# Two-layer image kernel: groups of 20, 7, 3 and 2 images instead of 21, 8 and 3, the last group's spectra kept on chip, and statistics sums started two rounds ahead

## The chip, the cores and the metric

The kernel runs on one core of a Trainium2 chip. The core has a matrix engine (TensorE, PE in the profile; PEld is its weight load), a vector engine (DVE), a scalar engine (ACT), GpSimd (POOL) and a queue engine for transfers (SyncE, SP).[...] The metric is the device time of one execution in microseconds (us); lower is better. The profile is one execution taken by the hardware profiler.

## The reference, cut to what matters

Two layers, each of the form x + f(normalised x), on 32 images of 32 channels of 128x128 numbers in float32.

```python
# layer 0: _gn normalises over groups of 2 channels; then, for each 128x128 matrix A,
Y = A / normA;  Z = I
for _ in range(5):
    T = 0.5 * (3.0 * I - Z @ Y);  Y = Y @ T;  Z = T @ Z
x = x + Y * sqrt(normA)
# layer 1: _gn again, then
x_dht = fftn(v, axes=(2, 3)).real
top = einsum('bixy,ioxy->boxy', x_dht[:, :, :32, :32], weights1)
bot = einsum('bixy,ioxy->boxy', x_dht[:, :, -32:, :32], weights2)
out_dht = zeros; out_dht[:, :, :32, :32] = top; out_dht[:, :, -32:, :32] = bot
x = x + ifftn(out_dht, axes=(2, 3)).real
```

Layer 0 is a matrix iteration on 1024 matrices. Layer 1 keeps 64x32 frequencies of a transform, mixes the 32 channels with a weight matrix of its own at each frequency (the weights are 8 MB in all), and transforms back.

## The kernel before

**Layer 0.** The unit of work is a set: 4 channels of one image, a tile of 128 partitions x (4 x 128). There are 8 sets to an image, 256 in all. `newton` (L393) is a generator that takes one set through its chain of products; one call of `products` (L297) is 4 matmuls of 128x128x128, recorded as 8 (two records to a float32 matmul). A set has 11 such calls, and `transposed` (L303), 4 transposes on TensorE, one to three times. For the images called far (`is_far`, L309: images 1 to 19) `quartic` (L357) does its transpose on DVE in blocks of 32 and through DRAM (the tile `turn`); for the near ones (0 and 20 to 31) it does it on TensorE. FIRST (L50), which sets the limit, is the first group's size less one.

**Rounds.** The main loop (L876) is written out at build time. In a round it goes once over 9 lanes (LANES); each lane holds a set and takes it on by one `yield`. A new set starts every 3 rounds (far) or 5 (near). The code of the engines' queues comes from the order in which this loop emits, rearranged by a planner except where an instruction is marked `kept`. Side queues of generators are stepped once a round or less: `preps` (statistics of the input for layer 0's normalisation, `prep` L180), `posts` (at lane 3: `settle` L419 stores a finished set to DRAM as `mid`, folds it on POOL and takes its moments; `forward` L436 transforms 8 folded tiles' rows on TensorE), `specs` (at lane 2: `spectrum` L475 does the column transform, the second layer's statistics through `moments` L157 and two matmuls at L509 and L512, and stores the scaled spectrum `spec` to `xs` in DRAM), `prods` (two rounds in three) and `backs` (the third).

**Layer 1's mixing.** Images are mixed in groups, GROUPS (L41), so that a weight that is loaded serves many images. When a group's last spectrum is done, `follow` (L859) queues its mixing on `prods` and its images' `inverse` (L726) on `backs`; a group's inverses begin when `prods` is empty (`finish`). The first group, of 21, is mixed by `wide_products` (L545), 32 steps of 16 matmuls that stream 128 columns. Groups of up to 8 go through `small_products` (L601): 16 steps (one for each kk, with its 512 KB of weights) of 32 matmuls that stream 32 columns, with the spectra read back from `xs` (L622), copies of the PSUM result to `om` (L667) and stores of it to `od` in DRAM (L631). A group smaller than 8 copies and stores `om` in four parts. `inverse` loads `od` (L688) and `mid` (tile `yt`, L703), reorders (L736), multiplies (L748, L770), copies the sine part to `d` (L782), adds on DVE (L787), adds and subtracts on POOL (L723), and stores the image (L711).

**The end.** When no set is left (`tail`), every queue is stepped at every lane, half of L723 goes to DVE, and the sets' tiles are released, so that 14 of the 16 weights can be loaded to tiles of their own by POOL's queue (L886).

**The statistics' waits.** In `moments`, `prep` and `spectrum` a small matmul sums over the partitions what DVE has just made: L167 (`ms`), L206 (`q` of `prep`), L509 (`qr`). Between DVE's instruction and the matmul stands one `yield`, so one round. `forward` has none between POOL's folds and its matmuls (L447) but the one at the end of `settle`.

## Time and profile before

| | |
|---|---|
| median of 3 runs | 3196.84 us (3196.34 to 3201.53) |
| span of the profiled execution | 3205.1 us, 78907 instructions |
| DMA | 637.55 MB, mean 199 GB/s |
| matmuls of the sets, L300 | 8 groups of the page's part 5, 2048 or 4096 records each |
| last L413, the end of layer 0's last set | begins 3081.36 us |
| column transform of images 0, 1, 18, 19, 20, 21 (L484 begins) | 159.6, 259.4, 1714.5, 1789.0, 1871.8, 1983.5 us |
| the same of images 26, 27, 28, 29, 30, 31 | 2555.2, 2669.8, 2777.2, 2895.5, 3004.5, 3088.1 us |
| `wide_products` on TensorE (L581) | 1895.8 to 2048.6 us |
| `small_products` of the group of 8 and of the group of 3 (L652) | 2803.5 to 2877.4 us; 3112.7 to 3149.9 us |
| inverses of the group of 21 begin (L748) | 2058 to 2736 us, one every 34 us |
| inverses of the group of 8 begin | 2888 to 3115 us |
| inverses of the group of 3 begin | 3161.7, 3171.7, 3184.8 us |

The columns of a profile line are read as follows. In the table of stretches: the stretch, its length, busy time and instructions of each engine, the granted TensorE clock as a share of full speed, the share of the DMA engines and the GB/s they moved. In the list of waits: who waited for whom, the us in total, how often, and the longest. In the chain of work that ended last: start, length, what. In the timeline: start, length, engine, line, operation, output and inputs, count, and in brackets the idle time before it with what ended it. Several waits for different engines overlap, and a wait of an engine that is not the bound costs nothing.

### The profile page before, as it was taken

The numbers are of one execution on the slowest core, as the hardware profiler recorded it, in microseconds if no ns is written. First come the engines' busy times: TensorE is split into PE (matmuls) and PEld (weight loads), VectorE is DVE, ScalarE is ACT, GpSimd is POOL, SyncE is SP. The second block draws the span as 40 slices with busy tenths as digits, with TensorE's granted clock in tenths as the row PEclk, the third lists the DMA queues.
The fourth block names the chain that finished last, engine by engine and source line by source line (L and its number), as shares of the span: only waits on it lengthen the run. The fifth ranks groups of instructions, "written<-read, shape, count | busy, mean of one in ns | idle before, by whom it ended". The sixth has DMA issues, their size and how long they took to land.

```text
span 3205.1 us, 78907 instructions
## 1 busy us (share of the span) xinstructions
PE 2973.7 (93%) x29440; PEld 2850.6 (89%) x29440; DVE 2316.5 (72%) x5158; ACT 1701.5 (53%) x4148; POOL 2003.6 (63%) x2314
## 2 busy tenths in 40 slices
PE   6999999999999999999999999999999898999964
PEld 6899989999999999999999998889888888998953
DVE  5777777778778877788777765677776776756645
ACT  3555556565556555656655454455455454536533
POOL 3566666667667766667666443476767666646742
PEclk9999999999999999999999999999999999999975
DMA  3566666666666666666665346766676566476577
GB/s 126 164 204 193 202 187 199 208 202 212 199 200 213 196 201 190 202 201 208 211 198 159 96 148 206 221 219 216 214 232 219 194 231 206 160 224 212 187 264 232
DMA packets 482317, 637.55 MB, mean 199 GB/s; under 512 B 97936, under 2 KB 263056, under 8 KB 481936
## 3 DMA queue, kind: packets, MB, share of 16 engines
q1 hardware_dynamic: 366592, 413.82, 40.6%
q10 hardware_dynamic: 113328, 211.34, 21.2%
q0 software_dynamic: 2016, 7.34, 0.6%
q8 instruction: 235, 3.85, 0.5%
q14 instruction: 146, 1.20, 0.1%
HBM read 398.75 MB, written 233.57 MB: 197 GB/s over the span
## 4 chain that ended last, share of the span: by engine, by line
PE 68%; DVE 12%; DMA 11%; issue 3%; POOL 3%; ACT 2%; SPq 1%; ACTq 0%; DVEq 0%; POOLq 0%
PE ps L300 55%; PE ps L306 6%; DMA xs<-in_xt 4%; DMA w<-turn 2%; DVE turn L366 2%; PE ps L770 2%; PE ps L447 1%; DVE v L275 1%; DVE a_st L195 1%; POOL yt L723 1%; DVE q L275 1%; DMA yt<-mid 1%; PE ps L748 1%; DVE yt L787 1%; PE ps L581 1%
## 5 line engine op out<-in xcount | busy, mean ns | idle before, releaser
L381 POOL TENSOR_TENSOR w<-w,r 128x512 f32<-128x512 f32 x304 | 386.5, 1275 | 352.0 <-DMA w<-turn 300.9
L300 PE MATMUL ps<-w,v 128*128 128x128 f32 x4096 | 556.2, 280 | 8.9 <-POOL w L381 3.6
L334 ACT ACTIVATE b<-b,a_off,a_scr 128x128 f32<-128x128 f32 x1024 | 470.1, 490 | 144.5 <-issue 48.6
L300 PE MATMUL ps<-y,q 128*128 128x128 f32 x4096 | 531.2, 278 | 11.8 <-ACT d L782 9.9
L300 PEld LDWEIGHTS ps<-w,v 128*128 128x128 f32 x4096 | 506.2, 195 | 13.3 <-POOL w L381 5.8
L300 PEld LDWEIGHTS ps<-y,q 128*128 128x128 f32 x4096 | 496.6, 195 | 16.0 <-ACT d L782 10.4
L426 POOL TENSOR_TENSOR fold<-xt 128x256 f32<-128x256 f32 x512 | 363.6, 730 | 217.7 <-DVE xt L413 194.4
L275 DVE SCALAR_TENSOR_TENSOR q<-ps,eye 128x512 f32<-128x512 f32 x512 | 349.2, 682 | 174.4 <-PE ps L300 168.6
L723 POOL TENSOR_TENSOR yt<-yt,d 128x512 f32<-128x512 f32 x238 | 299.9, 1287 | 177.6 <-ACT d L782 132.2
L341 POOL TENSOR_SCALAR x<-xt,a_nm,a_sc 128x128 f32<-128x128 f32 x720 | 315.5, 450 | 20.4 <-DVE a_n L224 20.4
L409 ACT ACTIVATE y<-ps,a_t_s 128x128 f32<-128x128 f32 x1024 | 291.3, 368 | 63.6 <-PE ps L300 63.1
L195 DVE BATCH_NORM_STATS2 a_st<-xs 128x6 f32<-128x128 f32 x1024 | 227.2, 279 | 134.3 <-DMA xs<-in_xt 133.7
L294 POOL TENSOR_TENSOR r<-mb,eye 128x512 f32<-128x512 f32 x104 | 132.5, 1274 | 304.4 <-ACT mb L269 298.9
L300 PE MATMUL ps<-x,b 128*128 128x128 f32 x2048 | 279.4, 280 | 5.7 <-POOL x L341 5.6
L269 ACT ACTIVATE t<-ps 128x512 f32<-128x512 f32 x256 | 152.5, 596 | 247.6 <-PE ps L300 240.6
L366 DVE STREAM_TRANSPOSE turn<-v 128x512 f32<-128x512 f32 x304 | 277.6, 913 | 5.3
L300 PE MATMUL ps<-m,q 128*128 128x128 f32 x2048 | 280.1, 281 | 0.5 <-DVE q L275 0.5
L300 PE MATMUL ps<-m,mb 128*128 128x128 f32 x2048 | 280.2, 281 | 0.1
L300 PE MATMUL ps<-y,t 128*128 128x128 f32 x2048 | 277.4, 279 | 2.7 <-ACT d L782 1.4
L300 PE MATMUL ps<-x,q 128*128 128x128 f32 x2048 | 277.8, 279 | 1.9 <-DVE q L275 1.9
L413 DVE TENSOR_TENSOR xt<-ps,xt 128x512 f32<-128x512 f32 x256 | 175.4, 685 | 143.6 <-PE ps L300 141.0
L300 PE MATMUL ps<-q,t 128*128 128x128 f32 x2048 | 275.6, 278 | 0.0
(124 smaller groups left out, 5827.2 us busy)
## 6 DMA issues: line engine op xcount, KB each, us to landing
turn<-turn SPq DMA_DIRECT2D x304, 256.0 KB
b<-in_x ACTq DMA_DIRECT2D x256, 256.0 KB
xt<-in_xt ACTq DMA_DIRECT2D x256, 256.0 KB
xs<-in_xt ACTq DMA_DIRECT2D x256, 256.0 KB
mid<-xt SPq DMA_DIRECT2D x256, 256.0 KB
yt<-mid SPq DMA_DIRECT2D x128, 512.0 KB
out<-yt SPq DMA_DIRECT2D x109, 512.0 KB
w<-turn SPq DMA_DIRECT2D x152, 256.0 KB
```

Of the source, the lines that this page charges most:

```text
L195: nc.vector.bn_stats(st[:, 4 * i + c, :], tiles[i][:, c, :])
L275: nc.vector.scalar_tensor_tensor(s, ps, f, t, ALU.mult, ALU.add)
L300: nc.tensor.matmul(ps[:, j, :], lhsT[:, j], rhs[:, j], start=True, stop=True)
L306: nc.tensor.transpose(ps[:, j, :], t[:, j, :], ident)
L334: nc.scalar.activation(t, x, AF.Identity, bias=offset[:, c], scale=scale[:, c])
L341: nc.gpsimd.tensor_scalar(m[:, j, :], xt[:, j, :], nm[:, c // 2 : c // 2 + 1], sc[:, c : c + 1], ALU.add, ALU.mult,)
L366: nc.vector.transpose(blocks(t), v.rearrange(form, b=4))
L381: nc.gpsimd.tensor_tensor(w, w, r, ALU.add)
L409: nc.scalar.mul(y[:, j, :], py[:, j, :], sn[:, c : c + 1])
L413: nc.vector.tensor_tensor(xt, products(t, y), xt, ALU.add)
L426: nc.gpsimd.tensor_tensor(f[:, :, 64 * half : 64 * half + 64], xt[:, :, 0:64], xt[:, :, 64:128], op)
L723: engine.tensor_tensor(yh, yh, d, op)
```

## The change

It has four parts.

1. **Groups.** GROUPS becomes (20, 7, 3, 2). The group of 3, mixed after the last set until now, is mixed while sets are still under way, and only two images are left for after. Image 19 becomes near, for FIRST falls from 20 to 19.
2. **The last group.** Its spectra don't go to DRAM. Eight copies, on ACT and DVE by turns, lay each `spec` out in `diags` as a stationary operand that is block-diagonal in l (4 blocks of 32 channels); 32 of its columns are 2 images x 4 values of l x 4 frequencies. `last_products` streams past them the weights of the same four frequencies at once, 4 x 32 columns: 128 matmuls of 128 columns instead of 512 of 32. Of the 4 x 4 pairs of frequencies that this forms, the stores pick the four that match. Its results are copied to `om`, stored in 16 transfers on two queues, and read back by `inverse`, which splits its reordering between ACT and DVE. It also loads the first of the two images' `mid` ahead.
3. **Late weights.** While the last set is under way, 28 half weights of 256 KB are loaded on SP's queue to tiles of the sets as these come free (`weights`, with the round from which each tile may be taken). The release of the sets' tiles and POOL's loads go.
4. **Sums two rounds ahead.** The one `yield` before L167, L206 and L509 becomes two. The second layer's statistics become a generator of their own, `summed`, that is queued right after the last `settle` of an image, ahead of `forward`; `spectrum` takes up its result. `forward` begins with a `yield`.

```diff
-GROUPS = (21, 8, 3)
+GROUPS = (20, 7, 3, 2)
...
         nc.vector.tensor_reduce(ms, f[:, :, :, 1], AX.X, ALU.add)
-        yield
+        yield from pause
         pm = bank()[:, 0, 0:G]
...
+    pause = (None, None)
...
-        yield
+        yield from pause
         pq = bank()[:, 0, 0:C]
...
     def forward(b, q, u):
+        yield
...
+    def summed(b, st):
+        ms, _, d = yield from moments(st, "b")
+        yield
...
+        yield from pause
+        pv = bank()[:, 0, :]
...
+        scales[b] = v, r
+        yield
...
+        v, r = scales.pop(b)
         ps = transposed(z)
...
+        if i == len(xs):
+            for e, t in enumerate(diags):
+                for l4 in range(4):
+                    rows = slice(32 * l4, 32 * l4 + 32)
+                    copy = nc.scalar.copy if l4 % 2 else nc.vector.tensor_copy
+                    copy(
+                        t.rearrange("p (m b l f) -> p m b l f", b=2, l=4, f=4)[rows, :, j, l4, :],
+                        spec[rows, 8 * e : 8 * e + 8].rearrange("p k q (h f) -> p (k q h) f", f=4),
+                    )
+            yield
+            return
...
+        if i == len(GROUPS) - 2:
+            for t in diags:
+                nc.gpsimd.memset(t, 0.0)
+            for kk in range(2):
+                load_weights(kk)
...
+    def last_products(i):
+        for e in range(2):
+            load_input(B - GROUPS[i], e)
+        for kk in range(KK):
+            if kk % 4 == 0:
+                yield
+                om = page(f"om{i}_{kk}").rearrange("p (f s o) -> p s f o", f=4, s=8)
+            if kk % 2 == 0:
+                pm = bank()
+            for h in range(2):
...
+                for q in range(4):
+                    m = 8 * (kk % 8) + 2 * q + h
+                    nc.tensor.matmul(
+                        pm[32 * q : 32 * q + 32, 2 * (kk % 2) + h, :],
+                        diags[kk // 8][:, 32 * m : 32 * m + 32],
+                        wt[:, q, :],
...
+            if kk % 4 == 3:
+                for f in range(4):
+                    queue = nc.scalar if f % 2 else nc.sync
...
+    def weights():
+        kinds = [("b", 2)] * 3 + [("x", 2), ("b", 4), ("x", 4), ("x", 10), ("y", 10), ("y", 10)]
+        kinds += [("m", 11)] * 2 + [("r", 12)] * 4 + [("mb", 15)] * 2 + [("v", 15)] * 2
+        kinds += [("w", 16)] * 2 + [("y", 16), ("m", 16), ("r", 17)] + [("q", 19)] * 3
...
-            if late and turn % 2:
-                y = late[0].tile([P, 8, P], F32, tag="yt_late", name=f"yt{b}_{o}", bufs=8)
+            if len(settled) == B * C // 4 and not folds and turn % 3 == 2:
+                y = sets.tile([P, 8, P], F32, tag="fold", name=f"yt{b}_{o}", bufs=3)
...
+            if where[b][0] == len(GROUPS) - 1:
+                for h, copy in enumerate((nc.scalar.copy, nc.vector.tensor_copy)):
...
+        if g == C // 4 - 1:
+            posts.append(then(summed(b, st)))
         if g % 4 == 3:
             posts.append(forward(b, g // 4, u))
...
-        if tail and not posts and not late:
-            phase.close()
-            late.append(ctx.enter_context(tc.tile_pool(name="late", bufs=1)))
-            for kk in range(2, KK):
-                late_wts.append(late[0].tile([P, 2, 4, 4, C], F32, name=f"wt{kk}_late"))
-                nc.gpsimd.dma_start(out=late_wts[-1], in_=wk[kk])
...
             step(norms)
+            step(loads)
...
+                if not todo:
+                    loads.append(weights())
```

## The prediction

> **What bounds the kernel now.** I read the page's busy shares, then a table of stretches, then TensorE's waits, then the chain of waits after layer 0's last set. The table of stretches first:

> ```profile
> 60.00:1680.00 1620.00, 1565.95 (x13867) 1519.38 (x13867) 1273.12 (x2862) 948.27 (x2343) 1087.37 (x1209) 0.98 0.64 198
> 1680.00:1900.00 220.00, 217.09 (x1990) 210.55 (x1989) 153.61 (x362) 111.36 (x269) 126.43 (x164) 1.00 0.39 119
> 2060.00:2800.00 740.00, 690.99 (x6637) 657.12 (x6635) 538.39 (x1168) 371.11 (x928) 504.96 (x594) 0.97 0.64 211
> 2880.00:3060.00 180.00, 174.12 (x1735) 165.54 (x1737) 115.92 (x212) 106.12 (x240) 121.92 (x140) 1.00 0.63 200
> 3082.00:3113.00 31.00, 7.90 (x88) 5.02 (x84) 10.36 (x25) 4.55 (x11) 12.39 (x19) 0.56 0.92 336
> 3113.00:3154.00 41.00, 21.31 (x1083) 19.12 (x1071) 20.23 (x28) 12.61 (x26) 5.44 (x4) 0.62 0.50 153
> 3154.00:3173.00 19.00, 8.14 (x74) 7.76 (x76) 3.10 (x5) 6.00 (x8) 0.98 (x1) 0.50 0.87 225
> 3173.00:3205.00 32.00, 11.74 (x122) 9.85 (x119) 27.33 (x32) 9.91 (x25) 16.65 (x12) 0.61 0.88 310
> ```

> There are two kernels here. Up to 3082 us PE (first busy figure) is 93 to 99% busy and its weight loads 89 to 96%, no other engine is over 79%: PE is the bound, so each us of PE work added costs about one, and each us of PE standing still that goes is about one gained. After 3082 PE is a quarter to a half busy, at little over half clock: the last 123 us are a chain of waits. What PE waits for between 60 and 3060 us:

> ```profile
> PE ps L206 <- DVE a_qs L201: 34.9, 16, 8.9
> PE ps L509 <- DVE b_qr L504: 14.9, 7, 3.1
> PE ps L447 <- POOL fold L426: 12.9, 7, 4.4
> ...
> PE ps L206 <- DVE b_r_q L150: 7.1, 2, 3.7
> PE ps L206 <- DVE b_inv L521: 5.2, 2, 3.2
> ```

> With two smaller rows (L206 4.4, L167 1.2) the statistics' matmuls and the folds hold PE for 80.6 us, out of some 125 us. The chain after the last set, its longest pieces:

> ```profile
> 3095.96 13.49 DMA xs<-spec
> 3114.96 1.57 SPq L622
> 3119.61 4.36 DMA diag<-xs
> ...
> 3129.39 6.84 DMA od<-om
> 3139.48 4.14 DMA od<-om
> ...
> 3159.80 12.91 DMA yt<-mid
> ```

> The spectra's way through DRAM takes from 3095.96 to the first product at 3112.73 (it shares the DMA engines with POOL's 7.3 MB of weights: 336 GB/s), the products to 3152.7, held by SP's loads and stores, then results and `yt` come back until 3172.7. The three images go at DVE's pace: `yt` L787 and L723 repeat every 11 us (3173.8, 3184.7, 3195.6).

> [...] The trace shows 0.50 to 0.62 in the tail, and the 24 records of L770 take 2.2 us there against 1.2 before. [...] In the trace 32 records of L581 (128 rows by 32, 128 columns) take 1.11 us, where 32 of L300 take 3.6, so three to four at once. [...]the 24 KB stores `od<-om` land in 1.5 us, which I use.

> **The change part by part, layer 0's stretch.**
> *Sums two rounds ahead.* A far round lasts 86 us / 24 = 3.6 us (an image every 86 us, 8 sets of 3 rounds), a near one 110 / 40 = 2.8. The mean wait is 51.6 / 22 = 2.3 us at L206, 2.1 at L509, 1.8 at L447. One round more covers nearly all of them (not the 8.9 us one). Behind the waiting matmul stands all of PE's queue, so the gain is direct, where PE has other work. DVE may still lag: bounds 30 and 80 us, I take 70%, **-56**. The added yield of `forward` hides in the spacing of sets, and `summed` ends about when the spectrum is through; no cost.
> *Image 19 near.* 16 more calls of `transposed`; eight records of L306 stand in the chain with 1.02 us, so 0.5 us a call, 8 us of PE. Against it a far image leaves PE idle 3% of 86 us, and image 20, near and without layer 1 beside it, took 82.8 us where images 1 to 18 took 86.4 each. Bounds 0 and 8, **+5**. DVE and POOL are relieved.
> *The group of 3 mixed earlier.* 16 steps of 64 records at 1.07 us (L652 at full clock): **+17**. Its loads, stores and copies, 16 x 0.58 us ACT and 16 x 0.69 DVE, the four-part copies of the group of 7, and one more pair of memsets (3.6 us POOL) lie on engines 60 to 75% busy: nothing.
> *Two more inverses before the end* (30 instead of 28): 1.09 + 2 x 1.19 us of PE each: **+7**.
> *The drain.* At 3068 to 3075 PE waited for `gt`, which stood on ACT behind L736's 5.7 us wait for `or<-od`. In the new order the group of 3's inverses end earlier: image 29 is 80 rounds before the end, 11 go to its spectrum, 26 to 16 product steps (2803 to 2877 us), 3 x 12 to the inverses. 7 are left. **-3**.
> Sum -30: the last L413 ends at 3052 instead of 3082.1.

> **The tail**, counted from that end (before: 123.0 us).
> *To the spectrum* it took 13.9. The fold no longer stands behind POOL's `yt` (0.9), and the scale is there when `z` is transposed (2.6 between that and L526): 10.4.
> *Lay-out in `diags`:* eight copies of 32x256, four each on ACT and DVE; the nearest row is `d` L782, 128x256, 384 ns: 1.8. At 12.2 (before: first product at 30.6).
> *Products:* 256 records. At 32 in 0.84 us (1.11 less one latency of 0.27) 6.7 us at full clock, 13.5 at half. They are dense[...]: 10. At 22.2. PSUM copies (16 halves, two engines) keep up. The weights, 7.3 MB at 250 to 336 GB/s or 22 to 29 us, are issued from the last set's start, some 40 us before its end: hidden.
> *Store and read back:* copy 0.7, issue 0.6, landing 1.5 to 3[...], 2.2: 25.7. Loads 1.2 to issue and, from 3154.5 to 3159.8, 5.3 with `yt` beside them, without 3: 29.9. L736 takes 1.92 whole, half on each engine 1.1: 31. `yt` of the first image is there.
> *Two images:* L748 2.1, `gt` 1.1, first L770 2.3, then 2 x 11 on DVE, 1 for its part of L736, the last L723 1.9, the last stores 4.6: 35. **66** in all, so **-57**. Bounds 58 and 80.

> Span 3052 + 66 = 3118. The profiled execution is 8.3 us above the median, so **3110 us**.

> **Rivals.** *A: the waits only move.* DVE is 73 to 79% busy[...]; its sums come behind `v`, `turn` and `yt`, and PE freed of one wait may meet another. For it: some twenty other kinds of waits stand in the list. Against: none sums over 12 us, and in 1680 to 1900 us PE is 99% busy. Then the main stretch gains nothing: 3110 + 56 = 3166. *B: work spills into the tail.* If an inverse takes 13 rounds, not 12, or the last half weights (those for `q` come only at round 19 of the last set's 23) land late, the tail keeps 10 to 25 us: about 3128. *C: slower.* `page` has three buffers for `om`, `d` and `or`, and more mixing now goes on beside inverses. In the tail of before ACT stood 5.7 us at `d` for `od<-om`. Were that so at each of the 16 store steps of the groups of 7 and 3, ACT and then PE would lose 91 us, and SP's queue, held by a half weight whose tile is not free, another 10 with the `mid` stores behind it: 3110 + 101 = 3211. Against it: by the cadences (20 inverses of 34 us; spectra 110 us apart) products and inverses overlap only some 30 to 60 us in all.

> **How the numbers follow.** My forecast 0.54, A 0.2, B 0.18, C 0.08. Low end: all waits recovered (-24) and the tail at 58 (-8): 3078. High end: A with a little of B, 3172. Faster by over 0.2% (below 3190): 0.91; within 0.2% 0.02; slower 0.07, from C and its near cases.

> **What would show it.** Right: PE's waits at L206, L509 and L447 sum to under 25 us between 60 us and the last L413; that L413 ends near 3052; no `xs<-spec` in the tail; the first product 12 us after it, the last 22 after; first L748 at 31; two images 11 us apart; end at 66. Wrong: PE as idle in 60 to 3040 us as before under other names (A); L748 of image 29 after the last L413, or products waiting for weights (B); ACT idle before `om` or `d` with a DMA as releaser between 2500 and 3000 us (C). The forecast also falls if TensorE stays at half clock and streams one column tile at a time in the products: 256 records at 0.22 us (twice the 0.11 of an L300 record in a full row) would be 56 us.

## The result and the profile after

The kernel after takes 3104.59 us in the median of 4 runs (3097.7 to 3112.25) against 3196.59 before: a ratio of 0.971 with a 95% interval of 0.9682 to 0.9737. The forecast was 3110 us. Its profiled execution spans 3098.6 us, of before 3205.1, so the trace shows 106 us where the medians show 92: that of before is of an execution some 8 us above the median, that of after of one some 4 us below. Executions of the kernel after lie up to 15 us apart, and differences below are taken from spans that end at a marked instruction.

That mark is the end of layer 0's last set: line L413 before, L420 after. It falls from 3082.1 to 3035.0 us (forecast 3052), and the tail behind it from 123.0 to 63.6 us (forecast 66). The table of stretches of the kernel after (stretch, length, busy us of PE, PEld, DVE, ACT and POOL with counts, granted clock, DMA share, GB/s):

```profile
60.00:1600.00 1540.00, 1519.98 (x13658) 1476.73 (x13657) 1250.88 (x2820) 927.98 (x2291) 1068.95 (x1191) 0.99 0.67 204
1600.00:1770.00 170.00, 166.98 (x1584) 161.18 (x1583) 114.02 (x256) 82.22 (x199) 88.80 (x122) 0.99 0.36 108
1935.00:2600.00 665.00, 634.05 (x6927) 603.02 (x6926) 514.36 (x1083) 343.52 (x856) 468.35 (x547) 0.99 0.71 233
3034.00:3048.40 14.40, 6.44 (x44) 3.87 (x43) 4.99 (x22) 4.27 (x10) 2.78 (x4) 0.63 0.78 290
3048.40:3062.00 13.60, 8.63 (x256) 8.39 (x256) 3.05 (x5) 2.93 (x6) 0.00 (x0) 0.88 0.20 41
3062.00:3070.90 8.90, 2.08 (x16) 1.79 (x16) 1.20 (x2) 2.00 (x2) 0.00 (x0) 0.50 0.81 209
3070.90:3098.60 27.70, 9.68 (x112) 8.25 (x112) 19.80 (x24) 7.14 (x21) 11.75 (x8) 0.56 0.50 199
```

In the far stretch PE is now 98.7% busy (96.7% before), and its granted clock is 0.99 instead of 0.98. In the tail the 41 us of products of before have become 13.6, in which the clock rises to 0.88. TensorE's waits from 60 us to the mark, of the kernel after:

```profile
PE ps L307 <- DVE w L282: 9.8, 7, 2.5
PE ps L307 <- DVE q L282: 7.9, 6, 2.9
PE ps L307 <- ACT d L893: 7.6, 3, 4.3
PE ps L307 <- POOL w L388: 7.5, 6, 3.8
PE ps L859 <- ACT ob L847: 6.4, 2, 4.3
...
PE ps L455 <- POOL fold L433: 1.0, 1, 1.0
...
PE ps L213 <- DVE a_qs L208: 0.8, 1, 0.8
```

The statistics' matmuls (L213 is L206 of before) and the folds (L455, before L447) held PE for 80.6 us and hold it for 2.0. But the whole list has fallen by 42 us only, from 127.7 to 85.3: other waits have grown, chiefly those for the sets' own `w` and `q`. Part of that comes with the new groups, which alone let TensorE stand 10 us longer (e2 below).

Some pieces of the chain of waits of the tail:

```profile
3046.14 1.18 ACT spec L541
...
3048.44 3.44 PE ps L723 x64
...
3060.04 2.16 DMA od<-om
...
3065.02 5.58 DMA yt<-mid
...
3084.49 2.48 DVE yt L898 x4
```

No `xs<-spec` stands in it any more: the first product (L723) begins 2.3 us after L541, which scales the spectrum, the last one is done at 3057.1, the results are back at 3067.3, and DVE works off the two images.

### The profile page after: what moved, and what is told of

Its sections match the earlier page's. It is cut to its first block, busy times and chain, and to the rows that moved or that the text cites. A ratio compares the mean times of both kernels' runs of the same rounds, so it can differ in the third digit from the quotient of the medians.

```text
span 3098.6 us, 79471 instructions
## 1 busy us (share of the span) xinstructions
PE 2948.7 (95%) x29760; PEld 2828.6 (91%) x29760; DVE 2340.0 (76%) x5178; ACT 1704.0 (55%) x4153; POOL 1998.0 (64%) x2312
## 3 DMA queue, kind: packets, MB, share of 16 engines
q14 instruction: 145, 1.19, 0.1%
## 5 line engine op out<-in xcount | busy, mean ns | idle before, releaser
L388 POOL TENSOR_TENSOR w<-w,r 128x512 f32<-128x512 f32 x288 | 366.3, 1276 | 324.3 <-DMA w<-turn 274.8
L827 POOL TENSOR_TENSOR yt<-yt,d 128x512 f32<-128x512 f32 x248 | 311.2, 1282 | 153.7 <-ACT d L893 116.0
L301 POOL TENSOR_TENSOR r<-mb,eye 128x512 f32<-128x512 f32 x112 | 142.7, 1274 | 311.3 <-ACT mb L276 298.8
L348 POOL TENSOR_SCALAR x<-xt,a_nm,a_sc 128x128 f32<-128x128 f32 x736 | 322.7, 451 | 19.5 <-DVE a_n L231 19.5
L373 DVE STREAM_TRANSPOSE turn<-v 128x512 f32<-128x512 f32 x288 | 262.0, 910 | 4.6
L307 PEld LDWEIGHTS ps<-m,q 128*128 128x128 f32 x2048 | 251.6, 193 | 10.7 <-DVE q L282 5.8
```

Source lines behind the costliest of these rows:

```text
L301: nc.gpsimd.tensor_tensor(r, mb, eye, ALU.add)
L307: nc.tensor.matmul(ps[:, j, :], lhsT[:, j], rhs[:, j], start=True, stop=True)
L348: nc.gpsimd.tensor_scalar(m[:, j, :], xt[:, j, :], nm[:, c // 2 : c // 2 + 1], sc[:, c : c + 1], ALU.add, ALU.mult,)
L373: nc.vector.transpose(blocks(t), v.rearrange(form, b=4))
L388: nc.gpsimd.tensor_tensor(w, w, r, ALU.add)
L827: engine.tensor_tensor(yh, yh, d, op)
```

## Experiments

Three quantities are needed for them that no view gives ready made. **Standing** is the length of the stretch from 60 us to the mark less TensorE's busy time. **Clock loss** is what the granted clock below 1 takes in it: over stretches of 5 us, the sum of 5 us x (1 - granted clock). What is left of the stretch is **work**, at full clock. In us:

| kernel | mark | standing | clock loss | work | tail |
|---|---|---|---|---|---|
| before | 3082.1 | 128.5 | 58.4 | 2835 | 123.0 |
| e1: before, two yields at the sums | 3010.1 | 83.3 | 34.0 | 2833 | 129.6 |
| e2: before, new groups | 3115.8 | 138.7 | 47.8 | 2869 | 101.0 |
| e9: before, image 19 near | 3074.2 | 119.8 | 49.5 | 2845 | 129.2 |
| after | 3035.0 | 86.5 | 27.2 | 2861 | 63.6 |
| e5: after again | 3043.5 | 90.5 | 30.7 | 2862 | 63.0 |
| e3: after, one yield at the sums | 3120.3 | 142.7 | 56.4 | 2861 | 62.2 |
| e7: after, no yield in `forward` | 3066.8 | 109.3 | 32.5 | 2865 | 63.4 |
| e12: after, two more rounds | 3023.5 | 80.6 | 18.7 | 2864 | 62.5 |

The work column supports the method: it hardly changes with the yields, and steps by some 30 us with the groups. Standing and clock loss overlap where the clock is low while TensorE stands, by 2 to 8 us in these traces, so work is too low by as much. Each row is one trace. Up to the mark, after, e4, e5, e6, e8, e10 and e11 differ by a few transfers at most, and over these seven the mark lies between 3032.8 and 3047.5 us, standing between 85 and 95 and clock loss between 25 and 34: smaller differences than these show nothing.

### e1 and e3: the sums alone, from both sides

```diff
# e1, in the kernel before, at L165, L204 and L507
-        yield
+        yield from pause        # pause = (None, None)
# e3, in the kernel after
-    pause = (None, None)
+    pause = (None,)
```

e1:

> The kernel before with one edit only: two yields instead of one ahead of L167, L206 and L509 (no other order, no forward yield). Theory (the standing of TensorE at the sums is the main stretch's gain, and comes back nearly whole): waits at L206, L509 and L167 fall from 68 us to under 10, TensorE idle in 60 to 3060 us falls by 35 or more, and its busy time at the same work falls by 10 to 30 us because the granted clock rises from 0.98 to 0.99; the time falls by 45 to 75 us, to 3122 to 3152. Rival (the waits only move, and the gain of layer 0's stretch came from the new groups): idle falls by under 15 us, the time is 3180 to 3195.

e3:

> The kernel after with pause = (None,), so one yield again ahead of the three sums; summed ahead of forward, and forward's yield, stay. Theory: the waits at the sums are back with 50 us or more, the granted clock falls to 0.98, the time rises by 40 to 65 us to 3145 to 3170. Rival (the new groups made the gain): under 15 us, 3105 to 3120.

e1 took 3141.42 us, 0.9811 of before (0.9786 to 0.9836), as the theory had it; e3 3190.75, 0.9974 (0.9959 to 0.9988), 20 us more than the top of its range. Taking the second yield out again gives back 86 us of the change's 92. TensorE's waits in e3:

```profile
PE ps L213 <- DVE a_qs L208: 46.8, 23, 8.2
PE ps L307 <- DVE w L282: 12.9, 7, 4.2
...
PE ps L498 <- DVE b_qr L493: 7.4, 5, 3.0
```

and in e1:

```profile
PE ps L307 <- ACT sw L465: 26.5, 18, 3.8
PE ps L448 <- POOL fold L427: 9.9, 8, 3.3
```

So the yields do what they were meant to. In e1 65 us of waits at the sums go, but the wait for `sw` (in `forward`) grows from 3.5 to 26.5 us, and standing falls by 45: a third of it moves. In e3 56 us of waits at the sums come back and standing rises by 56: in the order of the kernel after nothing moves. The mark falls by 72 us in e1 and rises by 85 in e3 (73 to 88 against the seven marks named above). Clock loss supplies most of the rest: 24 and 29. How a stand costs clock is seen in the kernel before, in TensorE's timeline and in stretches of 5 us (busy, count, granted clock, DMA share, GB/s):

```profile
635.76 0.61 PE L206 MATMUL ps<-a_qs,avg_mean 128*128 128x32 f32 x2 [3.19 <-DVE b_inv L521]
...
639.63 1.91 PE L300 MATMUL ps<-x,b 128*128 128x128 f32 x8
```

```profile
625.00:630.00 5.00, 5.00 (x47) 1.00 0.68 224
630.00:635.00 5.00, 2.57 (x24) 1.00 0.30 83
635.00:640.00 5.00, 4.24 (x20) 0.52 0.38 125
640.00:645.00 5.00, 5.00 (x38) 0.80 0.40 126
```

TensorE stands 3.19 us; its granted clock is then 0.50 for 6.8 us (635.15 to 641.98 us), and eight records of L300 take 1.91 us instead of 1.06. The two pieces below 1 lose 3.4 us of clock, nearly all of it on top of the 3.2 us of standing. Not every stand does this: of the 25 of 2 us or more in the stretch before, 24 were followed by half clock, of the 35 of 0.5 to 2 us only 2; after, 11 of 17 and 2 of 32. Over the whole stretch before, 36 of 604 such 5 us pieces are below 0.9; after, 19 of 595.

### e2: the groups alone

```diff
-GROUPS = (21, 8, 3)
+GROUPS = (20, 7, 3, 2)
```

> The kernel before with one edit only: GROUPS = (20, 7, 3, 2); the last two spectra still go through DRAM and the late weights still come on POOL's queue. Theory (the prediction's +29 us of TensorE work before the end is real): the last L413 ends 20 to 30 us later than 3082; the tail loses one image (11 us) and what spilled into it, and is 95 to 110 us long instead of 123; the time is 3195 to 3210, no gain. Rival (regrouping costs layer 0's stretch nothing, since far image 19 was as dear as a near one): the last L413 ends at 3080 to 3090 and the time is 3170 to 3185.

3223.71 us, 1.007 of before (1.0045 to 1.0096): slower by 0.7%, and by more than expected. The mark is 33.7 us later, work is 34 us more, and the tail, one image shorter, is 101.0 us. The new groups alone lose; they pay only with what the last group's new way takes off the tail, 39 us more (e3's tail of 62.2, with the same groups).

### e9: image 19 near

```diff
-        return 0 < b < FIRST
+        return 0 < b < FIRST - 1
```

> The kernel before with image 19 near (is_far up to FIRST - 1), nothing else. Theory (prediction: 8 us of TensorE work less what the far image stands idle): busy time of TensorE to the last L413 plus 7 to 8 us, that L413 0 to 10 us later, the time 3197 to 3210. Rival (near images beside nothing else are faster than far ones, as image 20's 82.8 us against 86.4 looks): the last L413 3 to 6 us earlier.

3214.88 us, above its range, and 1.003 of before (1.0006 to 1.0055), which is 2 to 18 us more. In the trace work is 10 us more, standing and clock loss together 18 less, so the mark came 8 us earlier, which is within the spread of marks of one kernel, and the tail was 6 longer. But this trace is of one of the three shortest of the twelve executions (3205 us). The work is about as priced (8 us). That a far image stands more is suggested by this one trace, not shown, and what image 19 costs in the end isn't settled.

### e4 and e6: late weights and the way through DRAM

```diff
# e4: in weights(), ahead of the loads; the yield after each load goes
+        while todo or any(lanes):
+            yield
# e6: in spectrum, ahead of the lay-out in diags
+            kept(nc.sync.dma_start(out=there, in_=spec.rearrange(flat)))     # a tile in DRAM
+            spec = sp.tile([P, 4, P], F32, tag="sp", name=f"back{b}", bufs=2)
...
+            kept(nc.sync.dma_start(out=spec.rearrange(flat), in_=there))
```

e4:

> The kernel after with its 28 half weights issued only once the last set has left its lane, all in a row. Theory (in the kernel after they are hidden behind the last set): 7.3 MB at 340 GB/s is 22 us and the last ones are wanted some 20 us after the last L413, so the products wait: they end 5 to 15 us later, 3110 to 3120. Rival (the early loads slow the last sets as much as they save): same as after, 3100 to 3108.

e6, and e5 as its base:

> The kernel after with each of the last two spectra stored to a tile in DRAM and loaded back before it is laid out in diags; all else as it is. Theory (the way through DRAM is worth little once 7 MB of weights no longer stand before it): a store and a load of 256 KB on idle DMA engines are 2 to 3 us each, so the tail grows by 5 to 7 us, where the prediction put the first product 18 us earlier. Rival (the DRAM way itself was the 13 us of before): plus 13 to 18 us.

> The kernel after, unchanged, as the base for the runs beside it. Expected: last L420 at 3030 to 3040 us of its span, a tail of 62 to 66 us, 0.971 of the kernel before.

e5 gave 3103.92 us, 0.9698 (0.9672 to 0.9724). e4 gave 3113.15 us, 0.9719 (0.9688 to 0.975), so the intervals overlap, but the tail of its trace is 80.7 us against 63.6, and TensorE's timeline says where (in brackets the idle time before, and what ended it):

```profile
3064.08 0.43 PE L723 MATMUL ps<-v,diag 128*32 128x128 f32 x8 [2.22 <-DMA v<-in_wk]
...
3072.81 0.66 PE L723 MATMUL ps<-q,diag 128*32 128x128 f32 x8 [1.19 <-DMA q<-in_wk]
```

From 3064 us on the products wait for half weights; they end 35.6 us after the mark instead of 22.1, and the stores follow. So in this trace hiding the weights is worth 17 us of tail, and in that of the kernel after no product waits for them. But the trace is of the slowest of e4's four executions (3121 us; two others took 3107), and by the medians e4 is 9 us longer: 17 is the upper end. e6 gave 3106.79 us, 0.971 (0.9685 to 0.9734): not to be told from e5 by the clock, but the tail is 68.2 us against 63.0, and its chain shows the way through DRAM at its own price:

```profile
3045.90 2.04 DMA there<-spec
3047.99 2.74 DMA back<-there
```

That is 5 us for both ways, where in the kernel before the store `xs<-spec` alone took 13.5 us beside 7.3 MB of weights. Keeping the spectra on chip is a small part of the tail's gain.

### e7: forward's yield

```diff
     def forward(b, q, u):
-        yield
```

> The kernel after without the yield at the start of forward. Theory (TensorE stood 12.9 us at the folds before, and each stand of 2 us also costs clock): waits at L455 (here L454) come back with 8 to 13 us, and the last L420 ends 8 to 18 us later. Rival (summed, now ahead of forward, already takes the place of that yield): no change over 3 us.

3129.31 us, 0.9781 (0.9756 to 0.9807), 25 us more than e5. TensorE's waits:

```profile
PE ps L313 <- ACT sw L471: 14.5, 13, 2.9
PE ps L454 <- POOL fold L433: 13.2, 10, 3.9
PE ps L307 <- ACT d L892: 13.0, 7, 4.3
```

The folds are back with the expected 13 us; `sw` and `d` rise too, so the mark moves by 23 to 32 us, more than expected. The prediction had put this yield at no cost and had counted its gain inside the 80.6 us; taken out alone, it costs 25 of the 95 us. The parts don't add up, for e3 alone costs 86.

### e8, e10 and e11: the last images

```diff
# e8 and e11
-            engine = nc.vector if tail and o % 16 else nc.gpsimd
+            engine = nc.vector if tail and o == 24 else nc.gpsimd
# e10 and e11: out stores on nc.sync; both images' mid loaded at the start of last_products
-            kept((nc.scalar if tail else nc.sync).dma_start(out=out[b, :, o : o + 8, :], in_=y))
+            kept(nc.sync.dma_start(out=out[b, :, o : o + 8, :], in_=y))
```

> The kernel after with one of four L827 pairs on DVE in the tail (o == 24) instead of two. Theory (DVE sets the pace of the last images, 11 us each, 5.0 at L898 and 5.6 at L827): DVE has 7.8 us an image, POOL 8.8, so an image takes 9 us and the tail is 3 to 5 us shorter. Rival (POOL becomes the bound, or the wait for d): no shorter, or longer by up to 3.

> The kernel after with the last images' stores on SP's queue instead of ACT's, and the mid of both last images loaded at the start of last_products. Theory (DVE's 10.6 us an image is the bound of the last 28 us): the L842 copies come 1 to 2 us sooner, for fewer loads stand beside or, and the tail is 1 to 3 us shorter. Rival (ACT's standing before d, 3.5 us twice, behind a store that waits for L827, is the bound): 4 to 7 us shorter.

> The same, and one of four L827 pairs on DVE instead of two (as in e8_unfold_share). Theory (in that run POOL and DVE were paced by d, whose copies stood behind ACT's stores): now POOL 8.8 us an image, the tail is 4 to 7 us shorter than that of after (63 us), the time 3096 to 3101. Rival: POOL's longer list ends later, tail 61 to 64 us.

They gave 3103.08 us (0.9695, 0.9669 to 0.9721), 3110.94 (0.9695, 0.9648 to 0.9743) and 3102.11 (0.9673, 0.9628 to 0.9719), with tails of 64.7, 64.9 and 63.3 us: nothing gained in any, where e8 and e10 were expected to shorten the tail and e11 by 4 to 7 us. In e8 ACT's copies to `d` stood behind its own stores, which waited for POOL:

```profile
ACT d L893 <- POOL yt L827: 5.8, 2, 3.1
```

In e11 that was gone and DVE was through with the two images in 16 us instead of 20, but POOL's twelve operations ended later than DVE, and `or` came 1 us later. The tail's last part is shared so closely by DVE, POOL and ACT that moving one piece didn't shorten it in these three.

### e12: the same remedy at two more places

```diff
         nc.scalar.copy(sw, ps)
-        yield
+        yield from pause
...
                     obs[b].rearrange("p (l t o) -> p o t l", l=4, t=8),
                 )
+                holding.append(b)
+                yield
+                holding.pop()
```

> The kernel after with one round more at two further stands of TensorE: between sw (L472) and its transposes in forward, and between L847's reordering of ob and its matmuls in the inverses of the groups of 7 and 3 (stepped in the next round). Theory (a stand costs its length and nearly half of it again in granted clock, and a round more removes it): the 6 to 15 us of waits at L313 for sw and L859 for ob go, the last L420 ends 8 to 20 us sooner than after's 3035 to 3047, the time is 3085 to 3100. Rival (by now the waits move: other engines' order is what TensorE waits for): these waits go, others come, the time stays within 5 us of 3104; the inverses, a round longer, may spill into the tail.

3091.45 us, 0.9654 of before (0.9628 to 0.968). Its six executions (3079.64 to 3096.84) all lie below the six of e5 (3099.59 to 3108.47), though the two intervals of the ratio touch. The wait for `sw` has left the list, that for `ob` is halved:

```profile
PE ps L862 <- ACT ob L847: 3.2, 2, 2.8
```

Some others are a little higher (`d` 9.5, `w` 11.8), and standing fell by 6 to 10 us. Clock loss fell by 8 to 12: 7 stands of 2 to 3 us are left, of 11 in the kernel after and 10 in e5. Mark, standing and clock loss all lie below the ranges of the seven traces named above. The mark is 11 to 20 us earlier, and the version beats both kernels by the median.

## Why the prediction was right, and where not

Direction and time came as forecast, and so did the tail: -57 was said and -59 measured. For layer 0's stretch -30 was said and -47 measured (-39 in e5). These -47 us are 26 of work more, 42 of standing less and 31 of clock loss less; the forecast had +29 for the groups, -59 for standing and nothing for the clock. That the time came within 6 us is partly luck: the forecast took the profiled execution to be 8.3 us above the median, and that of after lies 4 below, so that by spans it was 19 us off (3118 against 3098.6).

1. **Sums two rounds ahead, -56.** This is the term that was mis-sized. The mechanism is shown by e1 and e3: -72 and 85 us. "One round more covers nearly all of them" held: 80.6 us of waits became 2.0. "So the gain is direct, where PE has other work" was too small a sum. Standing itself moved by 45 us in e1, where a third of it came back at `sw` (rival A, in part), and by the forecast 56 in e3. But the stands had cost clock as well, 24 to 31 us in all, which the prediction left out: it had reckoned with half clock in the tail only, while the trace of before already showed a granted clock of 0.98 in the stretch. It had also put `forward`'s yield at no cost and no gain of its own, and without it 25 us are lost (e7).
2. **Image 19, the group of 3 and two more inverses, +29.** Work rose from 2833 to 2835 us to 2861 to 2865, by 26 to 32: as summed. e2 puts it at 34. Image 19's share was priced about right as work (10 us for 8); its net cost isn't settled.
3. **The drain, -3**, can't be told apart. The last inverse before the tail begins at 3012.8 us (L859), 22 us before the mark, and POOL's last L827 ends 0.5 us after it, so next to nothing spilled (rival B didn't happen).
4. **To the spectrum, 10.4.** It took 12.6. "The scale is there when `z` is transposed" was right, but the statistics' matmuls stand ahead of the column transform (L523 begins 7.3 us after the mark, 6.0 before): L498 waits 1.5 us for `b_qr`, and the transform stands behind it on PE.
5. **Products, from 12.2 to 22.2.** They ran from 13.5 to 22.1. The first 64 records took 3.44 us at a mean granted clock of 0.56, the other 192 some 5.2 at 1.00. That the clock would rise within the products was an estimate of mine: 10 us, between 6.7 at full clock and 13.5 at half. The weights were hidden: no product waited for one.
6. **Store and read back, to 31.** The results were reordered at 33.4: ACT's two stores of each four, 0.6 and 0.85 us to issue, stand between its copies.
7. **Two images, 35.** 30.3 from L859 on: DVE took 10.6 and 9.3 us for them. The reading that the way through DRAM had cost 18 us was too large as a cause: by itself it costs 5 (e6). That the rest was the weights beside it is argued, not shown, for no run of the kernel after has both. The sum of the step didn't change by that.
8. **Rival C**, ACT held by transfers of `om`, didn't come: from 2500 to 3000 us ACT waited 19.8 us for `or`, and under 2 for each other transfer.

What was not tried by itself: the new place of `summed` ahead of `forward`, the dense products without SP's loads and stores, and the first image's `mid` loaded ahead. If the parts add, the last two are the 15 us of the tail that one image less (22, e2), the weights (17, e4's trace) and the spectra (5) leave, or 23 with the 9 us of e4's medians.

## What to carry to other kernels

Where TensorE is the bound, list what it stands for by name, and give a matmul that needs another engine's small result one more slot of distance in the order of emission; a regrouping that shortens the tail can cost more in front than it saves, so price both sides at full clock. Count standing at about one and a half times its length (e1: 45 us of standing and 24 of clock), but as a mean: in the kernel before 24 of the 25 stands of 2 us or more were followed by half clock, of the 35 of 0.5 to 2 us only 2. After such a repair look at the list again: part of the standing may have moved (a third in e1), and the same remedy worked once more at two other places (e12).

## What the runs showed of the hardware that I had not expected

In the kernel before a stand of TensorE of 3.19 us in a stretch that is otherwise fully busy was followed by half clock (granted clock 0.52 and 0.80 in two pieces of 5 us), and so were 24 of the 25 stands of 2 us or more. The prediction had reckoned with half clock in the tail only. Over layer 0's stretch the clock loss was 58 us of the kernel before and 19 us of e12; of the 58, some 6 us fall in time in which TensorE stands.

| busy in the step | steps | the next one at half clock |
|---|---|---|
| under 40% | 25 | 25 |
| 40 to 50% | 16 | 10 |
| 50 to 65% | 26 | 3 |
| 65% and more | 1637 | 0 |

So what counted in these two traces is how much of a stand fell into one step. The kernel before has an example of each kind: the stand of 3.19 us from above, and one of 2.77 us at L206 that begins at 2279.12 us. In steps of the grid (length, busy us and records of TensorE, granted clock, DMA share, GB/s):

```profile
631.74:635.16 3.42, 0.83 (x8) 1.00 0.16 48
635.16:638.57 3.41, 2.81 (x14) 0.50 0.14 50
638.57:641.98 3.41, 3.41 (x18) 0.50 0.77 258
641.98:645.40 3.42, 3.42 (x32) 1.00 0.32 83
...
2276.97:2280.38 3.41, 2.15 (x20) 1.00 0.95 354
2280.38:2283.80 3.42, 1.91 (x17) 1.00 0.07 26
2283.80:2287.21 3.41, 3.41 (x33) 1.00 0.00 0
```

The first leaves TensorE 24% busy in one step, and two steps at a granted clock of 0.50 follow. The second is divided between two steps, 63 and 56% busy, and the clock stays at 1.00. As an estimate from these counts, a stand took the clock down in every case (25 of 25) when 2.05 us of it (60% of 3.41) fell into one step, and then cost at least 1.7 us (half of a step).
